# Layer 1 of a four-layer graph kernel: features in four column tiles of 32, scaling and score copies on ScalarE, the denominators' guard as a bias of ln

## The chip, the cores and the metric

The kernel runs on one core of a Trainium2 chip. The metric is device time in microseconds (us) of one execution, as the median over runs. A core has TensorE (matmuls, PE in the profile, with its weight loads as a row PEld), VectorE (DVE), ScalarE (ACT), GpSimd (POOL) and SyncE (SP). Matmuls write to PSUM[...].

## The reference

Four graph layers follow each other, each adding its result to x (8 graphs of 2048 nodes with 64 features), all over one adjacency matrix. The change touches layer 1, a graph attention:

```python
h = jnp.matmul(input, W)
s_src = jnp.matmul(h, a_src)
s_dst = jnp.matmul(h, a_dst)
e = jax.nn.leaky_relu(s_src[:, :, None] + s_dst[:, None, :], negative_slope=0.2)
attention = jax.nn.softmax(jnp.where(adj > 0.5, e, NEG_INF), axis=2)
return jax.nn.elu(jnp.matmul(attention, h))
```

`input` is the normed and rectified x. Layer 0 is another attention over hyperedges and neighbours, layers 2 and 3 are products with the adjacency matrix.

## The kernel before

The eight graphs are taken as four pairs p; a pair's 2 x 64 features fill the 128 partitions. The adjacency matrix stays on chip as 16 row tiles `aT[m]` (128 x 2048) for m = 0 to 15. Layer 1 writes the exponential of a leaky relu as a larger one of two products. So the unnormed attention between neighbour tile m and the nodes is one VectorE instruction, max(R, wd) times the adjacency tile, with a factor vd that is put into the features: `hS` is h times vd, and the denominators are sums of vd times the same tile.

`attend` does one half hf (1024 nodes) of one pair. For each m it makes two tiles `pt`, one per graph b2 (L1733, 128 x 1024, six buffers in rotation). `features` then multiplies them with `hS[:, m]` into the PSUM tile `o`: one call per graph and 512 columns, each with 64 output partitions, so two of them fill the 128 columns of the array. `sums` multiplies them with vd, repeated over 32 columns, into `dn`: four calls, each with 32 output partitions and its `tile_position`. Between the two stands `between(m)`. On even m the order is features, between, sums; on odd m it is the reverse, so that two blocks of the same kind meet at the border from one m to the next.

`between` inserts matmuls of the next pair's preparation, `neighbour_steps`: for each of four chunks of 512 nodes the mean and the variance (each a matmul with the matrix of averages), then twice `ph`, a product with `Wx` (W and the two score vectors, 132 columns) for two tiles of 128 nodes. From each ph ScalarE makes vd (L1593); VectorE copies the four scores to `sc` (L1594) and writes `hS` (L1595). The PSUM tile of ph is one of tag "h", with one buffer: the next ph waits until all three have read it. While the last pair attends, `between` inserts the front part of layer 2 instead (norms and the products `py`, whose high and low parts are made on ScalarE and VectorE, L1890 and L1891).

After the last m, VectorE reads dn, guarded by a maximum with 1e-30, into `ds` (L1742); ScalarE takes Ln and then Exp with scale -1 (L1743, L1744), which gives the reciprocals. They go through DRAM by POOL's queue (L1746, L1749) to be spread over the partitions as `den`. `end`, called from `between` at m = 3 of the next half, multiplies o with den (`res`, L1756), applies elu (two activations, then `e`, L1760) and adds the result to x in DRAM by an accumulating DMA (L1762). `dn` has one buffer, `o` two. `scores` loads R, the row of scores spread over the partitions, by SP's queue (L1696).

The order of TensorE's instructions is fixed in layer 1 (`kit.strict`, and all matmuls are recorded at L734); that of VectorE, ScalarE and the queues is set by a planner from the modelled times of the instructions.

Of the kernel before, what the change touches and what calls it, by code (L numbers as in the profile page):

```python
# [8 lines left out]
FP = mybir.dt.float32  # L9
FR = mybir.dt.float32r  # L10
AF = mybir.ActivationFunctionType
OP = mybir.AluOpType
# [4 lines left out]
P = 128  # L17
B, N, F = 8, 2048, 64
E = 64
NP = B // 2  # L20
NT = N // P
# [6 lines left out]
def half(b2):  # L28
    return slice(b2 * 64, (b2 + 1) * 64)


def cols(c, w=CW):
    return slice(c * w, (c + 1) * w)
# [3 lines left out]
def general(  # L37
# [355 lines left out]
    with ExitStack() as l1:  # L393
# [29 lines left out]
        with ExitStack() as s0:  # L423
# [47 lines left out]
            for ig in range(NCW):  # L471
# [7 lines left out]
                for b in range(B):  # L479
# [4 lines left out]
                    for w in range(2):  # L484
# [4 lines left out]
                        for z, mx in now:  # L489
                            softmax(z, mx)  # L490
                        pend = (i0, b, [z for z, _ in now])
            attend(*pend)

    xs.close()
# [128 lines left out]
class InOrder:  # L623


    def __init__(self, tc, engine):
        self.tc, self.engine = tc, engine
# [8 lines left out]
class Kit:  # L636


    def __init__(self, tc, t, pool):
        nc = self.nc = tc.nc  # L640
        self.sync, self.vector = nc.sync, nc.vector
        self.tc, self.t, self.strict = tc, t, False
        self.ident = pool.tile([P, P], FP, name="ident_f")
        make_identity(nc, self.ident)
        self.ones = pool.tile([P, F], FP, name="ones_f")
        nc.vector.memset(self.ones, 1.0)
        self.avg = pool.tile([P, P], FP, name="avg_f")
        nc.vector.memset(self.avg, 0.0)
        for b2 in range(2):
            nc.vector.memset(self.avg[half(b2), half(b2)], 1.0 / F)  # L650
        self.eps = pool.tile([P, 1], FP, name="eps_f")
        nc.vector.memset(self.eps, EPS)

        self.W1x = pool.tile([P, P + 4], FP, name="W1x")
        for k in ("W1v", "W1e", "W2", "Wvc", "Wec", "cb"):
            setattr(self, k, pool.tile([P, P], FP, name=f"{k}_f"))
        for k in ("b1", "b2c", "ivc", "b1c"):
            setattr(self, k, pool.tile([P, 1], FP, name=f"{k}_f"))

        self.bad = pool.tile([P, 7 + NT * NCW], FP, name="bad")  # L660
        nc.vector.memset(self.bad, 0.0)
# [70 lines left out]
    def mm(self, *args, **kw):  # L732

        one = self.nc.tensor.matmul(*args, **kw)  # L734
        if self.strict:
            self.tc.keep_in_program_order(one)
# [803 lines left out]
class Layer1:  # L1540
# [20 lines left out]
    def neighbour_steps(self, p):  # L1561


        kit, sb, ps, Wx = self.kit, self.sb, self.ps, self.kit.W1x
        nc, mm = kit.nc, kit.mm
        x1_dram, r_dram = self.x1_dram, self.r_dram

        keep = self.sb2
        sc = sb.tile([P, NT, 4], FP, tag="sc", name="sc", bufs=1)
        vd = keep.tile([P, NT, 2], FP, tag="vd", name="vd")  # L1570
        wd = keep.tile([P, NT, 2], FP, tag="wd", name="wd")
        hS = None
        for c in range(NCW):
            x = sb.tile([P, CW], FP, tag="x", name="x1", bufs=1)
            nc.sync.dma_start(out=x, in_=x1_dram[p, :, cols(c)])
            mean = ps.tile([P, CW], FP, tag="ln", name="mean")
            var = ps.tile([P, CW], FP, tag="ln", name="var")
            xc = sb.tile([P, CW], FP, tag="xc", name="xc")
            q = sb.tile([P, CW], FP, tag="q", name="q", bufs=1)
            hn = xc  # L1580
            for _ in kit.norm_steps(hn, x, mean, var, xc, q):
                yield
            if hS is None:
                hS = (self.sb2 if p % 2 else sb).tile([P, NT, P], FP, tag="hS", name="hS", bufs=1)
            for g in range(2):
                if g:
                    yield
                ms = slice(4 * c + 2 * g, 4 * c + 2 * g + 2)
                ph = ps.tile([P, 2, P + 4], FP, tag="h", name="ph")
                for k in range(2):  # L1590
                    j = 2 * g + k
                    mm(ph[:, k, :], hn[:, j * P : (j + 1) * P], Wx, start=True, stop=True)
                nc.scalar.activation(vd[:, ms, :], ph[:, :, P : P + 2], AF.Exp, scale=0.2)  # L1593
                nc.vector.tensor_copy(sc[:, ms, :], ph[:, :, P:])  # L1594
                nc.vector.tensor_tensor(  # L1595
                    hS[:, ms, :].rearrange("p t (b f) -> p t b f", b=2),
                    ph[:, :, 0:P].rearrange("p t (b f) -> p t b f", b=2),
                    vd[:, ms, :, None].to_broadcast([P, 2, 2, F]), op=OP.mult,
                )
            yield  # L1600
        nc.scalar.activation(wd, sc[:, :, 0:2], AF.Exp, scale=0.8)
        rs = sb.tile([P, 2, NT], FP, tag="rs", name="rs", bufs=1)
        nc.scalar.activation(rs, sc[:, :, 2:4].rearrange("p t b -> p b t"), AF.Exp, scale=-0.8)
        pr = ps.tile([2 * NT, P], FP, tag="h", name="pr")
        kit.turn(pr, rs.rearrange("p b t -> p (b t)"))
        rr = sb.tile([2 * NT, P], FP, tag="rr", name="rr", bufs=1)
        nc.vector.tensor_copy(rr, pr)
        nc.sync.dma_start(out=r_dram[p].rearrange("b (t n) -> (b t) n", n=P), in_=rr)
        yield hS, vd, wd
# [94 lines left out]
    def attend(self, aT, p, hS, vd, wd, hf, between):  # L1704


        kit, sb, ps = self.kit, self.sb2, self.ps2
        nc, mm = kit.nc, kit.mm
        s = cols(hf, HN)
        R = self.first or [self.scores(p, hf, b2) for b2 in range(2)]  # L1710
        self.first = None
        o = ps.tile([P, HN], FP, tag="o", name="o")
        dn = ps.tile([P, CW], FP, tag="dn", name="dn", bufs=1)

        def features(m, pts):
            for k in range(2):
                for b2 in range(2):
                    mm(o[half(b2), cols(k)], hS[:, m, half(b2)], pts[b2][:, cols(k)], start=m == 0, stop=m == NT - 1)

        def sums(m, pts):  # L1720
            for k in range(2):
                for b2 in range(2):
                    q = 32 * (2 * k + b2)
                    mm(
                        dn[q : q + 32, :], vd[:, m, b2 : b2 + 1].to_broadcast([P, 32]), pts[b2][:, cols(k)],
                        start=m == 0, stop=m == NT - 1, tile_position=(0, q),
                    )

        for m in range(NT):
            pts = []  # L1730
            for b2 in range(2):
                pt = self.pt.tile([P, HN], FP, tag="pt", name="pt")
                nc.vector.scalar_tensor_tensor(  # L1733
                    pt, R[b2], wd[:, m, b2 : b2 + 1], aT[m][:, s].bitcast(FP), op0=OP.max, op1=OP.mult
                )
                pts.append(pt)
            order = (features, sums)[:: -1 if m % 2 else 1]
            order[0](m, pts)
            between(m)
            order[1](m, pts)  # L1740
        ds = sb.tile([P, CW], FP, tag="res", name="ds", bufs=1)
        nc.vector.tensor_scalar_max(ds, dn, 1e-30)  # L1742
        nc.scalar.activation(ds, ds, AF.Ln)  # L1743
        nc.scalar.activation(ds, ds, AF.Exp, scale=-1.0)  # L1744
        rows = self.d_dram[hf]
        nc.gpsimd.dma_start(out=rows, in_=ds.rearrange("(q r) n -> q r n", r=32)[:, 0, :])  # L1746
        den = sb.tile([P, HN], FP, tag="den", name="den", bufs=1)
        for b2 in range(2):
            nc.gpsimd.dma_start(  # L1749
                out=den[half(b2), :].rearrange("p (k n) -> p k n", k=2),  # L1750
                in_=rows.rearrange("(k b) n -> b k n", b=2)[b2 : b2 + 1].to_broadcast([F, 2, CW]),
            )

        def end():
            r = sb.tile([P, HN], FP, tag="res", name="res", bufs=1)
            nc.vector.tensor_mul(r, o, den)  # L1756
            e = sb.tile([P, HN], FP, tag="den", name="e", bufs=1)
            nc.scalar.activation(e, r, AF.Relu, scale=-1.0)
            nc.scalar.activation(e, e, AF.Exp, scale=-1.0)
            nc.vector.scalar_tensor_tensor(e, e, -1.0, r, op0=OP.add, op1=OP.max)  # L1760

            nc.gpsimd.dma_start(out=self.x1_dram[p, :, s], in_=e, accum_op=OP.add)  # L1762

        return [lambda: None, lambda: None, end]
# [496 lines left out]
```

## Time and profile before

| | |
|---|---|
| median of 3 runs | 1951.25 us (1949.47 to 1952.59) |
| profiled execution, its own time | 1953.49 us |
| its span in the profile | 1951.7 us |
| busy: TensorE, VectorE, ScalarE, GpSimd | 1888.2, 1191.2, 437.4, 310.3 us |
| layer 1's attention | about 460 to 866 us of the span |

A row of the costliest groups gives line, engine, operation, output and inputs by the program's names, shape and count; then busy time, mean length of one in ns; then the idle time of the engine before them and what ended it. "128*64" is rows by columns of the array. A float32 matmul call leaves two records of MATMUL and two of LDWEIGHTS. Matmuls are pipelined, so a record's length is not what it costs: the distance from start to start is. A timeline gives start, length, engine, line, operation, and in brackets the idle time before. In the table by stage each engine's busy time within a stretch stands beside the stretch's length.

### The profile page before, as it was taken

To read this page: it belongs to the slowest core of one execution; us is meant where nothing else is said; L and a number is where in the kernel's file an instruction comes from. 1 tells how busy PE (TensorE), PEld (TensorE's weight loads), DVE (VectorE), ACT (ScalarE), POOL (GpSimd) and SP (SyncE) were. 2 spreads that over 40 slices of the span, in tenths; PEclk is the share of its full clock that TensorE was granted. 3 is DMA by queue.
4 is the path that set the end of the run, shared out by engine and by line. 5 is a ranking of instruction groups with operands and counts; after the bars stand their busy time and mean duration, and the time that the engine had idled before them with its cause. 6 is when DMAs were issued, how large, how long until landed. Compare 5 with 4: busy or idle time off the path is not lost.

```text
span 1951.7 us, 23508 instructions
## 1 busy us (share of the span) xinstructions
PE 1888.2 (97%) x9060; PEld 1141.7 (58%) x9060; DVE 1191.2 (61%) x1917; ACT 437.4 (22%) x923; POOL 310.3 (16%) x435
## 2 busy tenths in 40 slices
PE   7999999888999999999999999999999999999997
PEld 6877767423323232247775567765577755677653
DVE  8676499667899998973327652346723266523465
ACT  6322355564212110111220101301112201012100
POOL 4111187311000000000002110111200022101122
PEclk9999899999999999999999999999999999999999
DMA  7656385374121212214200112101022011121000
GB/s 211 174 177 180 121 249 148 97 200 82 41 62 40 61 43 55 65 23 116 60 22 25 30 43 71 49 10 30 24 74 59 22 25 30 43 71 49 5 19 12
DMA packets 86363, 142.43 MB, mean 73 GB/s; under 512 B 33801, under 2 KB 34057, under 8 KB 83569
## 3 DMA queue, kind: packets, MB, share of 16 engines
q1 hardware_dynamic: 65200, 83.86, 14.8%
q0 software_dynamic: 21040, 56.98, 12.0%
q8 instruction: 73, 1.20, 0.3%
q14 instruction: 50, 0.40, 0.1%
HBM read 106.85 MB, written 37.09 MB: 74 GB/s over the span
## 4 chain that ended last, share of the span: by engine, by line
PE 74%; issue 14%; DVE 4%; DMA 3%; POOL 3%; ACT 1%; SPq 0%; POOLq 0%; DVEq 0%; ACTq 0%
PE acc L734 33%; PE u L734 13%; PE o L734 6%; PE dn L734 3%; PE py L734 3%; PE pgs L734 2%; PE acc L1058 2%; PE pd L734 2%; PE var L734 1%; PE mean L734 1%; DMA iv<-ind_dram 1%; DMA at<-in_adjT 1%; DVE pt L1733 1%; PE pv L734 1%; PE pm L734 1%
## 5 line engine op out<-in xcount | busy, mean ns | idle before, releaser
L734 PE MATMUL acc<-aT,parts 128*128 128x512 f32 x1664 | 462.0, 421 | 0.0
L734 PEld LDWEIGHTS acc<-aT,parts 128*128 128x128 f32 x1664 | 306.6, 188 | 111.8 <-issue 51.3
L734 PE MATMUL u<-W3f,y 64*128 64x512 f32 x1024 | 243.2, 589 | 0.0
L1733 DVE SCALAR_TENSOR_TENSOR pt<-R,wd,aT 128x1024 f32<-128x1024 f32 x192 | 236.1, 1279 | 9.7 <-DMA R<-r_dram 4.7
L734 PE MATMUL o<-pt,hS 128*64 128x512 f32 x1024 | 237.2, 599 | 0.8 <-DVE pt L1733 0.6
L2136 DVE TENSOR_TENSOR pr<-u,embf 128x512 f32<-128x512 f32 x256 | 170.7, 688 | 110.2 <-PE u L734 103.2
L734 PEld LDWEIGHTS u<-W3f,y 64*128 64x128 f32 x1024 | 102.3, 187 | 118.0 <-issue 118.0
L734 PEld LDWEIGHTS o<-pt,hS 128*64 128x64 f32 x1024 | 68.4, 136 | 159.9 <-issue 149.2
L734 PE MATMUL u<-W3f,v 64*128 64x512 f32 x512 | 135.0, 596 | 0.0
L2148 POOL TENSOR_TENSOR fold<-fold 128x256 f32<-128x256 f32 x64 | 47.7, 746 | 498.4 <-DVE fold L2147 498.4
L734 PE MATMUL dn<-pt,vd 128*32 128x512 f32 x1024 | 123.1, 598 | 0.0
L1952 DVE TENSOR_TENSOR yb<-py,cb_f 128x512 f32<-128x512 f32 x32 | 22.1, 691 | 161.3 <-PE py L734 161.3
L1058 PE MATMUL acc<-at,Y 128*128 128x512 f32 x384 | 104.7, 415 | 0.0
L734 PE MATMUL acc<-aTl,parts 128*128 128x512 f32 x384 | 98.8, 395 | 0.0
L2140 DVE TENSOR_TENSOR pr<-pr 128x512 f32<-128x512 f32 x128 | 88.2, 689 | 2.2
L2042 POOL TENSOR_TENSOR bq<-bq,xp 128x512 f32<-128x512 f32 x16 | 20.6, 1289 | 430.1 <-ACT xp L2025 430.1
L1733 DVE SCALAR_TENSOR_TENSOR pt<-R,wd,aTl 128x1024 f32<-128x1024 f32 x64 | 79.8, 1282 | 12.4 <-PE dn L734 8.2
L734 PEld LDWEIGHTS u<-W3f,v 64*128 64x128 f32 x512 | 57.3, 186 | 49.6 <-issue 36.1
L734 PEld LDWEIGHTS acc<-aTl,parts 128*128 128x128 f32 x384 | 71.4, 188 | 16.2
L1058 PEld LDWEIGHTS acc<-at,Y 128*128 128x128 f32 x384 | 70.7, 194 | 14.6 <-issue 1.3
L734 PEld LDWEIGHTS dn<-pt,vd 128*32 128x32 f32 x1024 | 26.9, 108 | 80.9 <-issue 75.9
L1966 DVE TENSOR_TENSOR parts<-tp,parts 128x512 fp32r<-128x512 f32 x16 | 11.1, 692 | 85.7 <-ACT parts L1965 85.7
(354 smaller groups left out, 2688.6 us busy)
## 6 DMA issues: line engine op xcount, KB each, us to landing
at<-in_adjT POOLq DMA_DIRECT2D x32, 512.0 KB, 5.5
raw<-in_adjT SPq DMA_DIRECT2D x64, 256.0 KB, 3.4
aT<-in_adjT POOLq DMA_DIRECT2D x12, 1024.0 KB, 6.2
xp<-xd SPq DMA_DIRECT2D x45, 256.0 KB, 3.0
R<-r_dram SPq DMA_DIRECT2D x14, 512.0 KB, 3.8
hlo<-lo_dram POOLq DMA_DIRECT2D x18, 235.1 KB, 3.7
hhi<-hi_dram POOLq DMA_DIRECT2D x18, 235.1 KB, 3.4
hi_dram<-hi SPq DMA_DIRECT2D x16, 264.0 KB, 3.4
```

The source lines that it names most:

```text
L734: one = self.nc.tensor.matmul(*args, **kw)
L1058: mm(acc[p], Y[h][:, m, p, :], at[:, k, :], start=m + h == 0, stop=m == NT - 1 and h == 1)
L1733: nc.vector.scalar_tensor_tensor(pt, R[b2], wd[:, m, b2 : b2 + 1], aT[m][:, s].bitcast(FP), op0=OP.max, op1=OP.mult)
L1952: nc.vector.tensor_tensor(yb, py, bias[:, None, :].to_broadcast([P, 4, P]), op=OP.add)
L1966: nc.vector.tensor_tensor(lo, tp, hi.bitcast(FP), op=OP.subtract)
L2042: nc.gpsimd.tensor_add(bq, bq, xp)
L2136: nc.vector.tensor_tensor(a, u[h], emb[:, i, 8 * w : 8 * w + 8, None].to_broadcast([P, 8, F]), op=OP.mult)
L2140: nc.vector.tensor_add(pr[h], pr[h], a)
L2148: nc.gpsimd.tensor_add(fold[:, :, 0:2, :], fold[:, :, 0:2, :], fold[:, :, 2:4, :])
```

## The change

Four edits, all in layer 1. `features` makes four products of 32 output partitions per 512 columns, with `tile_position`, as `sums` has them. In `neighbour_steps`, which prepares pairs 1 to 3, the score copy moves from VectorE to ScalarE, and the one VectorE product that makes hS for two tiles becomes four ScalarE copies with a scale, each for one tile and one graph (128 x 64). The maximum with 1e-30 on VectorE goes; Ln reads dn and adds 1e-30 as its bias, from a new column `tiny`. Pair 0's preparation, which is a function of its own (`first_neighbours`), stays.

```diff
+        self.tiny = pool.tile([P, 1], FP, name="tiny_f")
+        nc.vector.memset(self.tiny, 1e-30)
...
                 nc.scalar.activation(vd[:, ms, :], ph[:, :, P : P + 2], AF.Exp, scale=0.2)
-                nc.vector.tensor_copy(sc[:, ms, :], ph[:, :, P:])
-                nc.vector.tensor_tensor(
-                    hS[:, ms, :].rearrange("p t (b f) -> p t b f", b=2),
-                    ph[:, :, 0:P].rearrange("p t (b f) -> p t b f", b=2),
-                    vd[:, ms, :, None].to_broadcast([P, 2, 2, F]), op=OP.mult,
-                )
+                nc.scalar.copy(sc[:, ms, :], ph[:, :, P:])
+                for k in range(2):
+                    m = ms.start + k
+                    for b2 in range(2):
+                        nc.scalar.activation(
+                            hS[:, m, half(b2)], ph[:, k, half(b2)], AF.Copy, scale=vd[:, m, b2 : b2 + 1]
+                        )
...
         def features(m, pts):
             for k in range(2):
-                for b2 in range(2):
-                    mm(o[half(b2), cols(k)], hS[:, m, half(b2)], pts[b2][:, cols(k)], start=m == 0, stop=m == NT - 1)
+                for q in range(0, P, 32):
+                    mm(
+                        o[q : q + 32, cols(k)], hS[:, m, q : q + 32], pts[q // F][:, cols(k)],
+                        start=m == 0, stop=m == NT - 1, tile_position=(0, q),
+                    )
...
-        nc.vector.tensor_scalar_max(ds, dn, 1e-30)
-        nc.scalar.activation(ds, ds, AF.Ln)
+        nc.scalar.activation(ds, dn, AF.Ln, bias=kit.tiny)
         nc.scalar.activation(ds, ds, AF.Exp, scale=-1.0)
```

## The prediction

> **What bounds the kernel now.** I read the page first, then the table by stage, then timelines. The page's first part says that TensorE is busy nearly throughout. Rows of the costliest groups say what the changed matmuls are: "o" are the features, "dn" the denominators, both 512 columns wide; 1024 records each are two per matmul call.
>
> ```profile
> PE 1888.2 (97%) x9060; PEld 1141.7 (58%) x9060; DVE 1191.2 (61%) x1917; ACT 437.4 (22%) x923; POOL 310.3 (16%) x435
> ...
> L734 PE MATMUL o<-pt,hS 128*64 128x512 f32 x1024 | 237.2, 599 | 0.8 <-DVE pt L1733 0.6
> L734 PE MATMUL dn<-pt,vd 128*32 128x512 f32 x1024 | 123.1, 598 | 0.0
> ```
>
> Layer 1's attention runs from 460 to about 866 us. The table by stage, cut where the denominators of each half are read (pair 1 shown), has TensorE busy 52.65 of 53.40 and 47.66 of 47.70 us; VectorE has about 9 us free per pair, ScalarE 85.
>
> ```profile
> core 0: us, PE busy (x) PEld busy (x) DVE busy (x) ACT busy (x) POOL busy (x), PEclk, DMA share, GB/s
> 563.90:617.30 53.40, 52.65 (x290) 16.21 (x286) 48.11 (x54) 10.26 (x19) 2.77 (x4) 1.00 0.21 45
> 617.30:665.00 47.70, 47.66 (x276) 13.80 (x277) 44.15 (x43) 5.80 (x11) 2.76 (x4) 1.00 0.24 62
> ```
>
> So TensorE is the bound here, with no idle to remove. But "busy" hides something, which the timeline of matmuls and that of weight loads show (columns: start, length, engine). From start to start, a block of 16 "o" records takes 555.17 - 551.59 = 3.58 us and one of 16 "dn" 557.02 - 555.17 = 1.85: 5.43 us for two steps of m.
>
> ```profile
> 551.59 3.65 PE L734 MATMUL o<-pt,hS 128*64 128x512 f32 x16
> 555.17 1.92 PE L734 MATMUL dn<-pt,vd 128*32 128x512 f32 x16
> 557.02 3.65 PE L734 MATMUL o<-pt,hS 128*64 128x512 f32 x16
> ```
>
> ```profile
> 742.68 0.20 PEld L734 LDWEIGHTS o<-pt,hS 128*64 128x64 f32 x4 [0.84 <-issue]
> 743.17 0.14 PEld L734 LDWEIGHTS o<-pt,hS 128*64 128x64 f32 x2 [0.29 <-issue]
> 743.60 0.14 PEld L734 LDWEIGHTS o<-pt,hS 128*64 128x64 f32 x2 [0.28 <-issue]
> 744.02 0.14 PEld L734 LDWEIGHTS o<-pt,hS 128*64 128x64 f32 x2 [0.28 <-issue]
> ...
> 746.27 0.16 PEld L734 LDWEIGHTS dn<-pt,vd 128*32 128x32 f32 x8 [0.81 <-issue]
> 746.72 0.13 PEld L734 LDWEIGHTS dn<-pt,vd 128*32 128x32 f32 x4 [0.30 <-issue]
> 747.15 0.13 PEld L734 LDWEIGHTS dn<-pt,vd 128*32 128x32 f32 x4 [0.30 <-issue]
> ...
> 748.12 0.20 PEld L734 LDWEIGHTS o<-pt,hS 128*64 128x64 f32 x4 [0.84 <-issue]
> ```
>
> Inside a block, two "o" records run side by side and the next two follow after 0.428 us (743.17, 743.60, 744.02); four "dn" run side by side, with the next four after 0.43 (746.72, 747.15). One round is 0.428 us either way. At each change of shape the weight loads come 0.8 us after the last ones instead of 0.3: nothing is loaded ahead across it. 8 rounds of "o" are 3.42 us, 4 of "dn" 1.71, together 5.14. The remaining **0.29 us is two changes of shape, 0.147 each**.
>
> **What the Trainium skill says.** "TensorEngine Tiling (Array Packing)", Key Properties: "Changing tiling mode (not just tile) drains the TensorE". The trace agrees as to place: 0.147 us at every change of shape, none where only m, the bank or the tile changes. "TensorE: Matmul & The Clock Gate", Part 2: weight loads are pulled ahead of running matmuls; seen inside blocks, not across changes. "ScalarE: Activation LUTs", What ACT_TABLE_LOAD costs: 186 ns plus 0.833 ns an element, some 93 ns more for a scale held in a column, 93 ns overlap back to back. Here 128x4 takes 171 ns and 128x512 630, which fits. Same page, Table sets: Copy is in every set and Ln and Exp share one, so no table load is added.
>
> **The change part by part.**
>
> 1. *Features in four tiles of 32 columns.* Per step of m four calls become eight (8 records become 16), but four run at once, so it is still 4 rounds, 1.71 us; the 1024 extra records cost nothing while feed keeps up (rival D). Weight loads of 32 columns take 0.11 us and hide under a 0.428 us round, as those of "dn" do. Features and denominators now have one shape. The code runs features, inserted work, denominators on even m and the reverse on odd m, so every change of shape lies where inserted work may stand. With a 128-column matmul there (mean, var, ph, pr, py) the array changes shape anyway and nothing is saved. I counted block transitions in the matmul timeline from 462 to 868 us: 41 go straight from "dn" to "o", 36 straight from "o" to "dn" (18 of 32 places in each of pairs 0 to 2, 23 in pair 3). 77 x 0.147 = **-11.3 us**, all on TensorE and on the path. Bounds: 0 if the drain has another cause, -12 if entering and leaving 128-column work gets a little cheaper too.
>
> 2. *The guard off VectorE.* ds L1742 (8 x 0.69 us) goes; Ln reads dn itself, about 0.69 us as other Ln's with a bias column. VectorE has slack, so the 5.5 us are worth nothing except where it had run ahead and stood waiting for the last sums. That is once inside the layer, at pair 3's start:
>
> ```profile
> 764.43 5.21 PE L734 MATMUL o<-pt,hS 128*64 128x512 f32 x16
> 764.57 0.69 DVE L1742 TENSOR_SCALAR ds<-dn 128x512 f32<-128x512 f32 x1 [3.83 <-PE dn L734]
> ...
> 766.51 0.19 PEld L734 LDWEIGHTS o<-pt,hS 128*64 128x64 f32 x2 [1.02 <-DVE pt L1733]
> 767.71 0.20 PEld L734 LDWEIGHTS o<-pt,hS 128*64 128x64 f32 x4 [1.01 <-DVE pt L1733]
> ```
>
> VectorE idles 3.83 us in front of ds, then the next half's pt come late: this "o" block takes 5.13 us from start to start, not 3.58, and one 12 us later 4.31, since VectorE has no lead left when res and e (2 x 1.22 us) fall due. 1.55 + 0.73 = **-2.3 us**. The score rows for that half had landed by 748, so nothing else holds pt there. Elsewhere the next late thing is the load of R (1.2 us of waiting at a boundary), and TensorE doesn't feel it: pt is one to two microseconds early. Behind the new wait, Ln on dn, stand on ScalarE the squares of the next norm; Ln waited before too, by way of ds, so this comes 0.7 us sooner, and with it the DMAs of d_dram and den on POOL's queue; no DMA is added or moved. At the layer's end the same ds delays py and the first parts: TensorE loses 0.58 us in the second py block (866.04) and 0.51 before acc (868.60); I take half, **-0.5** (0 to -1).
>
> 3. *Scaling and score copies to ScalarE.* 24 x (0.42 + 0.16) us leave VectorE: again only slack, but ph's bank is freed by these reads, and matmuls are in fixed order:
>
> ```profile
> PE ph L734 <- DVE hS L1595: 1.0, 2, 0.7
> ```
>
> (From the table of waits over layer 1: us in total, times, longest.) By block lengths TensorE loses 1.84 us at seven such places (0.82 at 579.7, 0.37 at 680.8, the rest 0.1 to 0.2), VectorE being behind with pt, e or res. On ScalarE four scalings of 128x64 are, by the page's prices, 186 + 53 + 93 - 93 = 0.24 us apart (estimate; the nearest rows, 128x4 at 0.17 and 128x128 at 0.28 us, agree): 0.96, with vd and the copy about 1.3 us from vd's start. The tightest pair of ph leaves 481.11 - 479.37 = 1.74. So it fits, except behind the two 1.06 us activations of an end(). I take **-1.0**; ends -1.8 and +2. ScalarE's total grows by 24 x 1.05 = 25 us over 400, with room. The four-byte column "tiny" costs one memset at the start, under layer 0's loads: nothing; uncovered, some 0.1 us.
>
> 4. *Does VectorE take over?* pt follow each other every 1.20 us, 2.40 per m, against 2.57 of the new TensorE. In pair 1 VectorE's 92.3 us fall to about 87 against 101 - 18 x 0.147 = 98.5. No.
>
> Sum: 11.3 + 2.3 + 0.5 + 1.0 = 15.1 us. The profiled execution took 1953.49 (span 1951.7), so 1938.4; the median of the runs is 2.24 lower, 1951.25, so **1936**.
>
> **Rivals.**
>
> A, the sum above: 1936, with its own bounds 1934 (12 + 2.3 + 1 + 1.8 off) to 1940 (11.3 + 2.3 - 2 off). Chance 0.66.
>
> B, the gap belongs to going from one output and weight tensor to another, not to shape. For: "o" and "dn" never meet in the same shape. Against: changes of bank and of m inside blocks cost nothing. Then only parts 2 and 3 remain: 1951.25 - 3.8 = 1947.5, at the edge of 0.2% (3.9 us), which is about what a measurement of this kernel can tell from no change. Chance 0.12.
>
> C, most changes vanish but VectorE or the R loads, 5.43 - 5.14 = 0.29 us nearer per two m, catch TensorE at the boundaries, or ScalarE frees ph late: half of the gain, about 1944. For: R's wait of 1.18 us at 561.51 stands 1.5 us before its pt is needed. Against: VectorE sheds 5 us a pair. Chance 0.14.
>
> D, slower: **instruction feed**. Two steps of m hold 64 loads and matmuls in 5.43 us now, 85 ns each; then 96, for which 5.14 us leave 53.5 ns. Above 5.43/96 = 56.6 ns each the long rows of small matmuls lose. The TensorE page (Part 2, step 2) gives about 62 ns a matmul if decoded in software; if that held for loads too, 96 x 62 = 5.95 us, +0.52 for each of 64 double steps: +33, less 3.8, so 1981. Against: layer 0's 36 pn matmuls, each with its load, follow every 100 ns, 50 ns each (3.91 us for 36 with their start), and bursts inside rounds come every 7 ns. But these rows are hardly longer than a queue. Chance 0.08.
>
> That the change doesn't do what it says can't be: its calls fix the shapes.
>
> **How the numbers follow.** Range: A and C reach from 1934 to 1944; I widen it to B's 1947.5 above and by as much, 4 us, below, where shorter drains around inserted work would lead: 1930 to 1948, leaving out D and little else. Faster by over 0.2%: A, C and nearly half of B, 0.86. Within: the rest of B, 0.06. Slower: D, 0.08.
>
> **What would show it.** In the changed profile: an "o" row of 2048 records in 128*32 with an "o" to "dn" to "o" row of 5.14 us for two m instead of 5.43; weight loads evenly 0.43 us apart across its seams; the ds and hS rows gone from VectorE and 96 short scalings of about 0.24 us on ScalarE; at pair 3's start no block above 3.5 us for two m of features; the attention from 460 to about 851 instead of 866. Rounds longer than 0.43 us would speak for D, seams of 0.15 us that stay for B, seams replaced by waits for pt or ph for C. Equal spans of attention would make the prediction wrong.

## The result, and the profile after

The changed kernel takes 1935.03 us in the median of four runs, against 1951.92 in four runs of the kernel before; the ratio is 0.990 with a 95% interval of 0.9877 to 0.9923. In a later comparison of more runs it was 0.9901 (0.9869 to 0.9933), 1929.5 against 1951.6 us. So it is faster by 15 to 24 us, by the first interval. The forecast was 1936 with a range from 1930 to 1948.

The profiled execution has a span of 1935.3 us, 16.4 less. The page's first part and the two rows of layer 1's attention:

```profile
PE 1868.5 (97%) x10084; PEld 1142.5 (59%) x10084; DVE 1176.9 (61%) x1862; ACT 460.1 (24%) x1043; POOL 310.9 (16%) x435
...
L736 PE MATMUL o<-pt,hS 128*32 128x512 f32 x2048 | 234.7, 593 | 1.7 <-DVE pt L1739 1.6
...
L736 PE MATMUL dn<-pt,vd 128*32 128x512 f32 x1024 | 122.4, 595 | 0.0
```

TensorE has 1024 records more and 20 us less busy time: 12 of them less in layer 1, where "busy" had held the seams, and 8 less in layers 2 and 3, of which more below. The table by stage for pair 1, cut at the same events as before (where the denominators are read):

```profile
564.08:616.46 52.38, 51.69 (x417) 15.69 (x410) 45.58 (x42) 14.63 (x44) 2.77 (x4) 1.00 0.21 46
616.46:662.41 45.95, 45.95 (x405) 14.27 (x409) 42.08 (x37) 8.79 (x27) 2.75 (x4) 1.00 0.24 62
```

98.3 us instead of 101.1, still with TensorE busy throughout; VectorE has gone from 92.3 to 87.7 and ScalarE from 16.1 to 23.4. The timeline of matmuls in a stretch with no inserted work:

```profile
546.67 1.90 PE L736 MATMUL dn<-pt,vd 128*32 128x512 f32 x16
548.38 3.62 PE L736 MATMUL o<-pt,hS 128*32 128x512 f32 x32
551.82 1.90 PE L736 MATMUL dn<-pt,vd 128*32 128x512 f32 x16
553.53 3.62 PE L736 MATMUL o<-pt,hS 128*32 128x512 f32 x32
```

From start to start: "dn" 548.38 - 546.67 = 1.71 us, "o" 551.82 - 548.38 = 3.44, together 5.15 for two steps of m. That is the bare twelve rounds of 0.428; both seams are gone.

**Where the time went.** I cut each profile at two matmuls that both kernels have: the first "o", and the first product acc with W1v, where layer 2 begins in earnest.

| us | to the first o | from there to acc with W1v (layer 1) | to the last matmul (layers 2 and 3) |
|---|---|---|---|
| before | 462.1 | 406.5 | 1071.3 |
| changed | 466.3 | 394.4 | 1063.0 |
| difference | +4.2 | -12.1 | -8.3 |

Layer 1 gave 12.1 us. Layers 2 and 3, which no edit touches, gave 8.3. The clock granted to TensorE was 1.00 in layers 1 to 3 of both profiles, so it is not what differs. The part ahead of layer 1 can't be told from chance: it lies anywhere from 456 to 469 us over the eleven profiles of this case, with and without the change, and two profiles of the changed kernel itself, 7.6 us apart in their spans, are 7.5 us apart in this part. The medians' 16.9 us, near the predicted 15.1, thus hide two things: a gain that was not in the sum, and a part of the sum that did not come.

The part that did not come is at the start of pair 3. In the kernel before, the first "o" block there was late by 1.55 us (the prediction shows it), and the one 12 us later by 0.73, behind a short wait of VectorE for den:

```profile
775.65 1.22 DVE L1756 TENSOR_TENSOR res<-o,den 128x1024 f32<-128x1024 f32 x1 [0.82 <-DMA den<-d_dram]
...
776.86 4.38 PE L734 MATMUL o<-pt,hS 128*64 128x512 f32 x16
...
781.17 1.12 PE L734 MATMUL mean<-xp,avg_f 128*128 128x512 f32 x2
```

In the changed kernel, TensorE first, then VectorE:

```profile
759.73 3.62 PE L736 MATMUL o<-pt,hS 128*32 128x512 f32 x32
763.16 1.90 PE L736 MATMUL dn<-pt,vd 128*32 128x512 f32 x16
...
768.31 1.90 PE L736 MATMUL dn<-pt,vd 128*32 128x512 f32 x16
770.03 1.90 PE L736 MATMUL o<-pt,hS 128*32 128x512 f32 x16
772.91 3.11 PE L736 MATMUL o<-pt,hS 128*32 128x512 f32 x16 [0.98 <-DVE pt L1739]
775.95 1.12 PE L736 MATMUL mean<-xp,avg_f 128*128 128x512 f32 x2
```

```profile
762.87 3.87 DVE L1739 SCALAR_TENSOR_TENSOR pt<-R,wd,aT 128x1024 f32<-128x1024 f32 x3
770.44 1.23 DVE L1761 TENSOR_TENSOR res<-o,den 128x1024 f32<-128x1024 f32 x1 [3.70 <-DMA den<-d_dram]
```

The wait for ds is gone, and the first "o" block is on time (763.16 - 759.73 = 3.43 us). VectorE runs ahead through four steps of m. Then it comes to res of end(), queued in front of the next pt, and stands 3.70 us, instead of 0.82, until den has made its way through DRAM. The 32 "o" records at 770.03 take 775.95 - 770.03 = 5.92 us instead of 3.44: 2.5 lost in one block, where two had lost 2.3 before.

### The profile page after: what moved, and what is told of

Same layout as the page of the kernel before. It is cut to its first block, busy times and chain, and to the rows that moved or that the text cites. A ratio compares the mean times of both kernels' runs of the same rounds, so it can differ in the third digit from the quotient of the medians.

```text
span 1935.3 us, 25629 instructions
## 1 busy us (share of the span) xinstructions
PE 1868.5 (97%) x10084; PEld 1142.5 (59%) x10084; DVE 1176.9 (61%) x1862; ACT 460.1 (24%) x1043; POOL 310.9 (16%) x435
## 4 chain that ended last, share of the span: by engine, by line
PE 73%; issue 15%; DMA 4%; DVE 3%; POOL 2%; ACT 1%; SPq 0%; POOLq 0%; DVEq 0%; ACTq 0%
PE acc L736 33%; PE u L736 15%; PE o L736 5%; PE py L736 3%; PE dn L736 2%; PE pd L736 2%; PE pgs L736 2%; PE acc L1060 2%; DMA iv<-ind_dram 1%; PE mean L736 1%; PE var L736 1%; DMA at<-in_adjT 1%; DVE pt L1739 1%; PE pm L736 1%; DMA den<-d_dram 1%
## 5 line engine op out<-in xcount | busy, mean ns | idle before, releaser
L736 PE MATMUL acc<-aT,parts 128*128 128x512 f32 x1664 | 455.8, 418 | 0.0
L736 PE MATMUL o<-pt,hS 128*32 128x512 f32 x2048 | 234.7, 593 | 1.7 <-DVE pt L1739 1.6
L736 PEld LDWEIGHTS o<-pt,hS 128*32 128x32 f32 x2048 | 64.7, 110 | 155.6 <-issue 144.7
L736 PEld LDWEIGHTS dn<-pt,vd 128*32 128x32 f32 x1024 | 30.8, 109 | 73.0 <-issue 69.0
```

## The experiments

**Theory.** The features' tiles remove the seams (S); the guard's wait only moves from ds to res (W); and the new column shifts what is allocated behind it, which changes the pace of layers 2 and 3 (P). Rivals: layers 2 and 3 differ by chance from run to run (V); VectorE's relief is what gained; the late pt belongs to VectorE's load and not to a wait.

### The column alone

```diff
+        self.tiny = pool.tile([P, 1], FP, name="tiny_f")
+        nc.vector.memset(self.tiny, 1e-30)
```

> The kernel before plus the column 'tiny' alone, which nothing reads. It shifts every tile allocated after it on that side by 32 bytes per partition (the column is padded), among them the operand 'parts' of the products acc in layers 2 and 3; the row tiles aT, allocated from the other side, stay. Theory P (placement): the 8.3 us that layers 2 and 3 lost in the changed kernel (1071.3 to 1063.0 us from the first product acc with W1v to the last matmul, 233.6 to 229.8 ns from one acc<-aT,parts to the next) come from this shift alone: layers 2 and 3 about 1063, acc at 229.8 ns, layer 1 unchanged at 406.5 us, in all about -8 us (1943.5). Theory V (they differ from one run to another): 233.6 ns and 1071 as before, 1951.

Measured: ratio 0.996 (0.9948 to 0.9971), 1944.5 against 1952.2 us, with layer 1 at 407.0 and layers 2 and 3 at 1063.8. From one acc<-aT,parts to the next it is 229.8 ns on average where it was 233.6 (leaving out distances over 300 ns, most of them two matmuls long). The rows of the costliest groups, before and with the column:

```profile
L734 PE MATMUL acc<-aT,parts 128*128 128x512 f32 x1664 | 462.0, 421 | 0.0
L734 PE MATMUL acc<-aTl,parts 128*128 128x512 f32 x384 | 98.8, 395 | 0.0
```

```profile
L736 PE MATMUL acc<-aT,parts 128*128 128x512 f32 x1664 | 455.9, 418 | 0.0
L736 PE MATMUL acc<-aTl,parts 128*128 128x512 f32 x384 | 98.4, 395 | 0.0
```

Same counts and shapes, 6.1 us less busy time in the first row; the changed kernel has 455.8. A column that nothing reads gives 7.7 us: P stands, V falls. All profiles agree: layers 2 and 3 took 1071.0 to 1071.3 us in the four kernels without a shift, and 1062.8 to 1063.8 us in the five profiles with a column of 32 bytes.

### The tiles alone

```diff
-                for b2 in range(2):
-                    mm(o[half(b2), cols(k)], hS[:, m, half(b2)], pts[b2][:, cols(k)], start=m == 0, stop=m == NT - 1)
+                for q in range(0, P, 32):
+                    mm(
+                        o[q : q + 32, cols(k)], hS[:, m, q : q + 32], pts[q // F][:, cols(k)],
+                        start=m == 0, stop=m == NT - 1, tile_position=(0, q),
+                    )
```

> The kernel before with the features in four tiles of 32 alone. Theory S (seams): the array's changes of shape are worth 11.7 us; layer 1 from the first o to the first product of layer 2 goes from 406.5 to about 395, two steps of m from 5.43 to 5.15 us; layers 2 and 3 stay at 1071; in all about -12 us (1940). The place at the start of pair 3 keeps its 2.3 us of late pt. Rival R (VectorE had little lead left without the other two edits): pt or hS late more often, layer 1 at 398 to 402.

Measured: 0.9962 (0.9944 to 0.9979), 1943.1 us; layer 1 at 397.9, layers 2 and 3 at 1071.2. So 8.5 us in layer 1: R was right about the size (its 398 to 402, at the lower edge). The seams are gone, but TensorE, now faster, waits more for VectorE. Timeline of matmuls in pair 1:

```profile
574.23 1.92 PE L734 MATMUL dn<-pt,vd 128*32 128x512 f32 x16
577.51 0.69 PE L734 MATMUL ph<-W1x,xc 128*128 128x132 f32 x4 [1.36 <-DVE hS L1595]
```

The second ph stands 1.36 us until VectorE has written hS; in pair 2 it is 1.46 us, and pair 3 still starts late. This is what the scaling on ScalarE is for: with these two edits together layer 1 takes 394.6 us (the kernel without the guard's edit, below).

### The scaling and score copies alone

```diff
-                nc.vector.tensor_copy(sc[:, ms, :], ph[:, :, P:])
-                nc.vector.tensor_tensor(
-                    hS[:, ms, :].rearrange("p t (b f) -> p t b f", b=2),
...
+                nc.scalar.copy(sc[:, ms, :], ph[:, :, P:])
+                for k in range(2):
+                    m = ms.start + k
+                    for b2 in range(2):
+                        nc.scalar.activation(
+                            hS[:, m, half(b2)], ph[:, k, half(b2)], AF.Copy, scale=vd[:, m, b2 : b2 + 1]
+                        )
```

> The kernel before with the scaling of features and the score copies on ScalarE alone. Theory S: only the 1.8 us in which ph waited for VectorE can go, and ScalarE may add waits of its own: layer 1 at 404.5 to 407, layers 2 and 3 at 1071, in all -2 to +1 us (1949 to 1952). Theory that freeing VectorE is what gained: -5 us or more in layer 1.

Measured: 0.9995 (0.9983 to 1.0006), 1950.3 us, not told from no change; layer 1 at 404.7. The 1.8 us of ph's waits are gone, as much as was there, and the relief of VectorE by itself is worth no more. The rows of the changed kernel show ScalarE's price:

```profile
L1600 ACT ACTIVATE hS<-ph,vd 128x64 f32<-128x64 f32 x96 | 22.3, 316 | 0.0
L1596 ACT COPY sc<-ph 128x8 f32<-128x8 f32 x24 | 3.8, 160 | 0.0
```

22.3 us for 96 scalings is 0.23 us each, back to back; the record of one is 0.316 us long, so they overlap. The prediction had 0.24.

### The guard alone

```diff
+        self.tiny = pool.tile([P, 1], FP, name="tiny_f")
+        nc.vector.memset(self.tiny, 1e-30)
...
-        nc.vector.tensor_scalar_max(ds, dn, 1e-30)
-        nc.scalar.activation(ds, ds, AF.Ln)
+        nc.scalar.activation(ds, dn, AF.Ln, bias=kit.tiny)
```

> The kernel before with the column tiny and Ln reading dn with it as bias; features in halves and scaling on VectorE. As predicted on record, the late pt at the start of pair 3 would go: layer 1 at about 404. Theory W (the wait moves: without ds VectorE runs ahead to res and waits there for den): the o block there keeps 2 us or more over its 3.58, layer 1 at 406 to 407.5. By theory P layers 2 and 3 are at 1063 since the column is there. In all -8 (W) or -10 us.

Measured: 0.9944 (0.9925 to 0.9963), 1940.0 us; layer 1 at 404.7, layers 2 and 3 at 1062.9. Neither theory as it stood: layer 1 gained 1.8 us, between them. At the start of pair 3 VectorE stands at res (its timeline, then TensorE's):

```profile
775.49 1.22 DVE L1757 TENSOR_TENSOR res<-o,den 128x1024 f32<-128x1024 f32 x1 [3.32 <-DMA den<-d_dram]
```

```profile
775.86 1.94 PE L736 MATMUL o<-pt,hS 128*64 128x512 f32 x8
777.96 3.13 PE L736 MATMUL o<-pt,hS 128*64 128x512 f32 x8 [0.16 <-DVE pt L1735]
781.01 1.12 PE L736 MATMUL mean<-xp,avg_f 128*128 128x512 f32 x2
```

The first late block (1.55 us) is gone, but the second takes 781.01 - 775.86 = 5.15 us, 1.57 over its 3.58, where it had lost 0.73. So the wait has moved as W says, and the place costs 1.6 us instead of 2.3. And of TensorE's losses in front of ph, 1.84 us before, about 0.6 is left, probably because VectorE comes to hS sooner without the eight ds. Of the edit's 12 us in the medians the profile gives layer 1 1.8 and, by the column, layers 2 and 3 8.4; the other 2 are within the interval.

### The guard's edit left out of the changed kernel

The edit is that of the section above, taken back: maximum on VectorE, no column.

> The changed kernel without the edit of the guard: the maximum on VectorE is back, and with it the column tiny is gone. By theories S and W the guard's edit is worth nothing in layer 1 (its wait only moves from ds to res), and the scaling on ScalarE is what keeps the tiles' full gain (tiles alone: 397.9): layer 1 at 394 to 395, layers 2 and 3 at 1071 with acc<-aT,parts at 233.6 ns, about 1940 in all. If the guard's edit is worth the 2.3 us of the prediction on record, layer 1 is at 396 to 397.

Measured, in a single execution of 1934.8 us (456.1 of it ahead of layer 1, the shortest of all): layer 1 at 394.6, layers 2 and 3 at 1071.0, acc<-aT,parts at 233.8 ns. With the other two edits in place the guard's own edit is worth 0.2 us in layer 1, less than two profiles of the changed kernel differ by (394.4 and 394.1), and the column the rest. The three edits, each alone, give 8.5 + 1.8 + 1.8 = 12.1 us in layer 1, exactly what they give together; that is chance, since tiles and scaling together already give 11.9.

### Later end()

```diff
-        return [lambda: None, lambda: None, end]
+        return [lambda: None] * 4 + [end]
```

> The changed kernel with end() called two steps of m later, at m = 5 instead of 3. Theory W: in the changed kernel VectorE, free of ds, runs ahead to res and stands there until den has landed (9.0 us in 6 waits), which makes pt late at the start of pair 3 (an o block of 5.92 us instead of 3.43) and xc and ph late in pair 1 (0.7 us). Two steps later den is there first: the o block at the start of pair 3 at 3.4 to 3.6 us, layer 1 from the first o to layer 2's first product at 391 instead of 394.4, in all about -3 us against the changed kernel. Rival (VectorE is simply too slow there, res and e falling due in any case): layer 1 stays at 394.

Measured: 0.9887 (0.9861 to 0.9913), 1927.7 us, beside 1929.5 and 0.9901 for the changed kernel on the same chip. By the intervals the two can't be told apart, but the profile can tell them: layer 1 at 391.1 instead of 394.4 and 394.1. The start of pair 3:

```profile
755.09 3.62 PE L736 MATMUL o<-pt,hS 128*32 128x512 f32 x32
758.52 1.90 PE L736 MATMUL dn<-pt,vd 128*32 128x512 f32 x16
760.24 3.62 PE L736 MATMUL o<-pt,hS 128*32 128x512 f32 x32
763.78 1.13 PE L736 MATMUL mean<-xp,avg_f 128*128 128x512 f32 x2
```

Each "o" is at 3.4 to 3.5 us. From the table of waits over layer 1, the changed kernel and this one:

```profile
DVE res L1761 <- DMA den<-d_dram: 9.0, 6, 3.7
```

```profile
DVE res L1761 <- DMA den<-d_dram: 3.4, 4, 1.6
```

W stands: the late pt was a wait, not VectorE's load. No block of "o" or "dn" is late any more, apart from the very first. This kernel has the shortest median of the study.

### The changed kernel again

> The changed kernel once more, beside the others on one chip. Expected: 12 us of layer 1 and 8.3 us of layers 2 and 3 together, 0.990 of the time before, about 1932 to 1935; layer 1 at 394.4 and layers 2 and 3 at 1063 in the profile, layer 0 at 460 to 468 as chance has it.

Measured: 0.9901 (0.9869 to 0.9933), 1929.5 us; layer 1 at 394.1, layers 2 and 3 at 1063.0, layer 0 at 458.8.

### Which shift counts

Two kernels. The changed one with a column of 64 bytes:

```diff
-        self.tiny = pool.tile([P, 1], FP, name="tiny_f")
+        self.tiny = pool.tile([P, 9], FP, name="tiny_f")
...
-        nc.scalar.activation(ds, dn, AF.Ln, bias=kit.tiny)
+        nc.scalar.activation(ds, dn, AF.Ln, bias=kit.tiny[:, 0:1])
```

> The changed kernel with tiny nine columns wide (only the first is used), so that it takes 64 bytes instead of 32 and everything behind it lies 64 bytes from its place before. Theory P64 (it is the address modulo 64 that counts): layers 2 and 3 back at 1071, acc<-aT,parts at 233.6 ns and acc<-aTl,parts at 231.3; layer 1 stays at 394; in all about +8 us against the changed kernel (1943). Rival (any shift away from the place before helps): 1063 and 229.8.

and the one before with 32 bytes put ahead of the pool of pt and parts:

```diff
+        pad = self.lasting.enter_context(tc.tile_pool(name="att_pad", bufs=1, reuse_waits="tile"))
+        nc.vector.memset(pad.tile([P, 1], FP, name="att_pad"), 0.0)
         self.pt = self.lasting.enter_context(tc.tile_pool(name="att_pt", bufs=6, reuse_waits="tile"))
```

> The kernel before with 32 bytes put just ahead of the pool of pt and parts: parts lie 32 bytes on, as in the changed kernel, but the row tiles aTl (the last four) stay in their place; the other row tiles aT stay in all kernels. Residues modulo 64 of parts, aT, aTl: 32, 32, 0 (before 0, 32, 0; changed 32, 32, 32). Theory own (the place of parts alone counts): 229.8 ns for both acc<-aT and acc<-aTl, layers 2 and 3 at 1063. Theory pair (moving and stationary operand should have the same residue): 229.8 for aT, 233 for aTl, layers 2 and 3 at about 1065. Layer 1 at 406 to 407 in either.

Measured: with 64 bytes 0.993 (0.9905 to 0.9955), 1936.3 us, 7 more than the changed kernel beside it where 8 were expected (their intervals overlap, so it is the profile that decides), layers 2 and 3 back at 1069.9, layer 1 at 393.6. With parts shifted, but not aTl (a single execution of 1953.2 us, 468.5 of it ahead of layer 1), layers 2 and 3 took 1065.1 us and layer 1 406.2. Its rows, then those of the 64-byte column:

```profile
L734 PE MATMUL acc<-aT,parts 128*128 128x512 f32 x1664 | 455.6, 418 | 0.0
L734 PE MATMUL acc<-aTl,parts 128*128 128x512 f32 x384 | 99.4, 397 | 0.0
```

```profile
L736 PE MATMUL acc<-aT,parts 128*128 128x512 f32 x1664 | 460.8, 420 | 0.0
L736 PE MATMUL acc<-aTl,parts 128*128 128x512 f32 x384 | 98.7, 395 | 0.0
```

Together: start addresses modulo 64 (as the expectation above gives them; the two columns shift by 32 and by 64 bytes) and the mean distance between starts in ns:

| kernel | parts | aT | aTl | acc<-aT | acc<-aTl | layers 2 and 3, us |
|---|---|---|---|---|---|---|
| before | 0 | 32 | 0 | 233.6 | 231.3 | 1071.3 |
| column alone | 32 | 32 | 32 | 229.8 | 230.1 | 1063.8 |
| changed | 32 | 32 | 32 | 229.8 | 229.8 | 1063.0 |
| 64-byte column | 0 | 32 | 0 | 233.2 | 231.0 | 1069.9 |
| parts shifted, not aTl | 32 | 32 | 0 | 229.5 | 232.7 | 1065.1 |

A shift of 64 bytes undoes the gain, so not any move helps. And moving parts without aTl makes the products with aT faster and those with aTl slower. That is theory "pair": a product is faster when the row tile and parts have the same residue. It is not all, since with both at 0 it is 231.3 ns and with both at 32 about 230. Residues other than 0 and 32 were not tried, and why placement counts no run shows.

## Why the prediction was right or wrong

The total lay in the range and 1 us from the forecast, but that it came so near is luck: layer 1 gave 12.1 us and not the 15.1 of the sum, and 8.3 came from layers for which the sum had nothing. By the sum:

- **Part 1, seams, -11.3.** Right in mechanism and size. In the kernel with the later end(), which has no late block but the first, layer 1 is 406.5 - 391.1 = 15.4 us shorter than before; the late blocks of the kernel before, 1.84 + 1.55 + 0.73, make 4.1 of that; 11.3 remain for the seams. Two steps of m went from 5.43 to 5.15 us; rival B (tensor and not shape) is out, since "o" and "dn" still alternate. The tiles alone show some of rival C: 2.8 of the 11.3 us came back as other waits.
- **Part 2, guard, -2.3 at the start of pair 3.** Wrong. The failing step is "so nothing else holds pt there": I had looked at R and not at res, which stands in VectorE's queue and waits for den. The 1.55 us of the first block did go. But with ds gone VectorE reached res earlier, 3.70 us before den instead of 0.82, and the second block, whose 0.73 was to go too, lost 2.5; so the place costs as much as before, and the sign "no block above 3.5 us" did not come. The wait that comes next belongs in the price of a wait removed.
- **The layer's end, -0.5.** Wrong, and the same loss counted twice: the 0.51 before acc lies inside the 0.58 by which the second py block is long. Nothing of it went. The block still takes 860.73 - 858.17 = 2.56 us, and acc still waits for VectorE's parts. These follow py through ScalarE (from 859.36) and VectorE (from 859.98), and ScalarE had done with ds 3.5 us before:

```profile
858.17 2.05 PE L736 MATMUL py<-W1e_f,v 128*128 128x128 f32 x16
860.73 1.12 PE L736 MATMUL acc<-v,W1v_f 128*128 128x512 f32 x2 [0.51 <-DVE parts L1896]
```

- **Part 3, scaling, -1.0.** About right, though in another way: the 1.84 us in front of ph went, and a new 0.7 came in pair 1, where ph waits for xc after VectorE had stood 1.97 us at res; the second profile of the changed kernel has no such wait in pair 1 but a late block of 0.7 us in pair 3. Beside the tiles the edit is worth more than alone, 397.9 - 394.6 = 3.3 us, since with the tiles ph waits longer for hS. ScalarE's price of 0.24 us was met by 0.23.
- **The column "tiny", nothing.** Wrong: it is worth 8.3 us, by placement. I priced its memset and not its 32 bytes. Without it the total would have been about 12 us, 1939, still in the range.
- **Rival D, the feed.** Out. 96 loads and matmuls in 5.15 us, 54 ns each, without a longer round. Part 4 holds too: VectorE fell to 87.7 us in pair 1, as predicted (87), under TensorE's 98.3 (98.5).

## What to carry to other kernels

A TensorE that is busy all the time can still have time to give: compare start to start with the bare rounds, and look for changes of array shape; give neighbouring products one shape where that costs no rounds. When a wait is taken off an engine's queue, ask what it runs into next, and move that too (end() two steps later). And when a change adds even a small buffer, look at the stages that it should not touch: placement alone was worth 0.4% here, and would have been booked to the edit that brought it.

## What was not expected of the hardware

For the products acc of layers 2 and 3 (128x512), operands whose start addresses in a partition differ by 32 modulo 64 took 3.8 ns more a matmul than those that are both at 32 (233.6 against 229.8 ns). With both at 0 it was 231.3. Over the 2560 records of acc with a row tile that made about 8 us.
